# A decoder whose cross attention moves row centring and probability copies to ScalarE and forms its query projection from seven half-size products

## The chip, the cores and the metric

The kernel runs on one core of a Trainium2 chip, in float32 throughout. The metric is the device time of one launch in microseconds (us). Engines are named as in the profile: PE (TensorE: matmuls and transposes; PEld its weight loads), DVE (VectorE), ACT (ScalarE), POOL (GpSimd) and SP (SyncE, whose queue issues every DMA of this kernel).

## The reference, cut to what matters

An encoder layer works on a context of 2 x 77 rows of 512; a decoder layer then works on 2 sequences of 2048 rows of 512, with 16 heads of 32 and a feed-forward width of 2048.

```
y = y + mha(ln1(y), ln1(y), sa_*, causal + relative bias)   # self attention
y = y + mha(ln2(y), memory, ca_*, relative bias)            # cross attention, 77 keys
h = ln3(y)
y = y + relu(h @ ff1_w.T + ff1_b) @ ff2_w.T + ff2_b
```

with `ln(x) = (x - mean) * rsqrt(var + eps) * s + b` on each row, and inside `mha`: `q = (xq @ wq.T + bq) / sqrt(32)`, scores, softmax, times v, output projection. The change lies in the cross attention: how `ln2` and `ln3` centre a row, how its softmax probabilities are brought into the turned layout, and how its `q` is multiplied.

## The kernel before, in words

The rows of the decoder are cut into 8 blocks of 512 (2 sequences x 4), a block into 4 tiles of 128 rows. Every engine's order of work is the order in which the program issues it: nothing is reordered.

The first part, up to about 1757 us, runs 128 units of self attention, with the encoder and the cross attention of block 0 (`first_cross`, slots 65 and on) laid between them in `light`, `late` and `jobs` lists by unit number. `w1_sums` and `w1_store` (L1125, L1137) form sums of quarters of the first feed-forward weight there on POOL, in four units of block 6, and write them to DRAM as `w1_d`.

The second part runs the feed-forward network of blocks 0 to 7. Both of its products are done by halves: a product of 2 x 2 halves takes seven products of halves instead of eight, on sums formed before, and adds them up in PSUM. Such an order is written in `ONE` (L1159): for each of the seven, the weight's half or sum, the half or sum of the rows, the chain of PSUM banks (0 or 1), whether the chain starts afresh, and the output quarter that it then holds. A block has 56 slots (`ff_slot`, L1364): 28 of `first_product` (L1294; 4 matmuls of 128x256) and 28 of `second_product` (L1323; 8 matmuls of 128x128, 4 in every fourth slot). An fp32 matmul is two records in the trace. Slot 0 begins with `sums_n` (L1225), four POOL subtractions of 128x512; `sums_h` (L1260) forms the sums for the second product on DVE and POOL. Weights are streamed by `feed` (L1200) into a ring of 16 places of 256 KB, `w_ring` (L1197), as many tiles ahead as it has places.

Beside the slots of block x, one step ahead of each slot, runs the cross attention of block x + 1 (`cross`, L1386). A list `plan` holds what is issued at each of the 56 steps; so at step n PE, DVE, ACT and POOL first get the entries of `plan[n]`, then slot n. With the stages named as in the code:

- Normalisation `n2` of tile t (`norm_stages`, L732): `stats` at step t (DVE, then the power -1/2 on POOL, L743), `center` at step t + 2 (DVE subtracts the mean and multiplies, L749; POOL then adds a bias row to y, L750), `turned` at step t + 4 (4 transposes on PE, L755, into one bank; 4 activations on ACT scale, shift and copy out, L758).
- The query projection, at steps 9 to 12: `q_group` (L762), 4 matmuls of 128x512 into one bank and one DVE operation (L766) each.
- Attention of tile t, beginning at step 14 + 7t - 1 or 14 + 7t (`attend_stages`, L768): `score` (16 matmuls into 4 banks; DVE subtracts the maximum), `exp` on ACT (L793), `sums` on DVE, `normalize` on POOL (L804), `turned` (L806: four groups of 4 transposes, each group into a bank that is copied out, the even ones by ACT, L814, the odd ones by DVE, L812), `times_v`, `out`. The score of tile 3 is at step 35, one after `turned` of tile 2.
- Normalisation `n3` of tile t, the same three stages, at steps 27, 29 and 31 (+ 7t).

This work takes its PSUM banks in turn from four (`bank`, L179); the feed-forward products have the other four. The cross attention of block 1 begins with its first steps between the last units; those of blocks 2 to 7 run beside the slots of blocks 1 to 6; block 7 has none beside it.

Of the kernel before, what the change touches and what calls it, by code (L numbers as in the profile page):

```python
# [10 lines left out]
F32 = mybir.dt.float32  # L11
AF = mybir.ActivationFunctionType
# [42 lines left out]
def tile_encoder_decoder(ctx: ExitStack, tc: tile.TileContext, ins, out):  # L55
# [5 lines left out]
    def wchunk(name, c0, n=D):  # L61

        return ins[name][:, c0 : c0 + n].rearrange("(c p) o -> p c o", p=P)
# [94 lines left out]
    with (  # L158
# [573 lines left out]
        def norm_stages(y, n, row, place, done):  # L732

            keep = {}

            def stats():
                st = sm.tile([P, 6], F32, name="bnst", tag="bnst")
                mv = sm.tile([P, 2], F32, name="cmv", tag="cmv", bufs=4)
                rs = sm.tile([P, 2], F32, name="crs", tag="crs", bufs=4)
                nc.vector.bn_stats(st, y())  # L740
                nc.vector.bn_aggr(mv, st)
                nc.vector.tensor_scalar_add(rs[:, 0:1], mv[:, 1:2], EPS)
                nc.gpsimd.tensor_tensor(rs[:, 1:2], rs[:, 0:1], mhalf[:, 0:1], ALU.pow)  # L743
                keep.update(mv=mv, rs=rs)

            def center():
                xn = keep["xn"] = place()
                mv, rs = keep["mv"], keep["rs"]
                nc.vector.tensor_scalar(xn, y(), mv[:, 0:1], rs[:, 1:2], ALU.subtract, ALU.mult)  # L749
                nc.gpsimd.tensor_tensor(y(), y(), row, ALU.add)  # L750

            def turned():
                xn, pt, dst = keep["xn"], bank(), done()
                for c in range(NC):
                    nc.tensor.transpose(pt[:, ts(c, P)], xn[:, ts(c, P)], ident)  # L755
                for c in range(NC):
                    sc, bi = vec(f"dec_{n}_s", c), vec(f"dec_{n}_b", c)
                    nc.scalar.activation(dst[:, c, :], pt[:, ts(c, P)], AF.Identity, bias=bi, scale=sc)  # L758

            return stats, center, turned  # L760
# [7 lines left out]
        def attend_stages(q, kTc, v, y, biased, pr, pts, place, w_o, bi=None):  # L768


            prh = pr.rearrange("p (h k) -> p h k", k=S)
            by_r = pr.rearrange("p (g r k) -> p g r k", r=HC, k=S)
            keep = {}

            def score():
                mx = sm.tile([P, NC, HC], F32, name="cmx", tag="cmx", bufs=3)
                banks = [bank() for _ in range(HC)]
                for g in range(NC):
                    for r in range(HC):
                        nc.tensor.matmul(  # L780
                            banks[r][:, ts(g, S)], q(g)[rows4(r)], kTc[rows4(r), g, :], start=True, stop=True
                        )
                for r in range(HC):
                    s = banks[r][:, : NC * S].rearrange("p (g k) -> p g k", k=S)
                    d = by_r[:, :, r, :]
                    if biased:
                        nc.vector.tensor_tensor(d, s, bi[r] if bi else d, ALU.add)
                        s = d
                    nc.vector.tensor_reduce(mx[:, :, r], s, AX.X, ALU.max)
                    nc.vector.tensor_tensor(d, s, mx[:, :, r, None].to_broadcast([P, NC, S]), ALU.subtract)  # L790

            def exp():
                nc.scalar.activation(pr, pr, AF.Exp)  # L793

            def sums():
                su = sm.tile([P, H], F32, name="csu", tag="csu", bufs=2)
                ri = sm.tile([P, H], F32, name="cri", tag="cri", bufs=2)
                nc.vector.tensor_reduce(su, prh, AX.X, ALU.add)
                nc.vector.reciprocal(ri, su)  # L799
                keep["ri"] = ri  # L800

            def normalize():
                ri = keep["ri"]
                nc.gpsimd.tensor_tensor(prh, prh, ri[:, :, None].to_broadcast([P, H, S]), ALU.mult)  # L804

            def turned():  # L806
                for g in range(NC):
                    pt = bank()
                    for r in range(HC):
                        nc.tensor.transpose(pt[:S, ts(r, P)], prh[:, g * HC + r, :], ident)  # L810
                    if g % 2:
                        nc.vector.tensor_copy(pts(g), pt[:S, :])  # L812
                    else:
                        nc.scalar.copy(pts(g), pt[:S, :])  # L814

            def times_v():
                ot = bank()
                for g in range(NC):
                    for r in range(HC):
                        h = g * HC + r  # L820
                        nc.tensor.matmul(
                            ot[rows4(r), ts(g, P)], v[:, ts(h, HD)], pts(g)[:, ts(r, P)], start=True, stop=True
                        )
                keep["oT"] = place()
# [200 lines left out]
        oflat = oT_all.rearrange("p a q -> p (a q)")  # L1025
        pr = oflat[:, : H * S]
        kTcs = [pts_all[:, 4 + b, : NC * S].rearrange("p (c k) -> p c k", k=S) for b in range(B)]
        w_q, vcs, qT = [], [], []

        def big(i):  # L1030
            return vflat[:, i * TB * D : (i + 1) * TB * D]
# [11 lines left out]
        def early_loads():  # L1043
            nc.sync.dma_start(nTt, nT3_d)
            row_into(bv, "dec_ca_out_b")
            for o in range(2):
                w_q.append(small_w(o * P, "dec_ca_in_wT"))
            w_q.append(pts_all[:, 6, :].rearrange("p (c o) -> p c o", c=NC))

        def last_loads():  # L1050
            t = sb.tile([P, MB], F32, name="q", tag="q", bufs=3)
            t = t.rearrange("p (c o) -> p c o", c=NC)
            nc.sync.dma_start(t, wchunk("dec_ca_in_wT", (NC - 1) * P, P))
            w_q.append(t)
            for b in range(B):
                t = sb.tile([P, MB], F32, name="q", tag="q", bufs=3)
                nc.sync.dma_start(t[:S, :], cv_d[:, b, :])
                vcs.append(t)

        def late_loads():  # L1060
            nc.sync.dma_start(w_q[2], wchunk("dec_ca_in_wT", 2 * P, P))
            for t in range(TB):
                new_y(1, t)
            for b in range(B):
                nc.sync.dma_start(kTcs[b], ckT_d[:, :, ts(b, S)])
            for _ in range(2):
                t = sb.tile([P, HC, 2 * P], F32, name="bias", tag="bias", bufs=2)
                qT.append(t.rearrange("p (g a) k -> p g (a k)", g=2))
# [7 lines left out]


        w1_d = dram.tile([4, NC, P, D], F32, name="w1_d")
        w2_d = dram.tile([7, 7, P, D], F32, name="w2_d")
        free = pp[:, 3 * HC * MB : END - 3 * HC * MB]  # L1080
        tens = free.rearrange("p (z q o) -> p z q o", z=8, q=2)
# [40 lines left out]
            for k in range(4):  # L1122
                store(z0, z1, f"T{k + 1}", t[:, k])

        def w1_sums(n):  # L1125

            raw = free[:, : 4 * D].rearrange("p (r k o) -> p r k o", r=2, k=NC)
            got = free[:, 4 * D :].rearrange("p (s k o) -> p s k o", s=4, k=2)
            for r in range(2):
                nc.sync.dma_start(raw[:, r], wchunk("dec_ff1_wT", r * (DFF // 2) + n * TOK, TOK))  # L1130
            a11, a12, a21, a22 = (raw[:, r, 2 * c : 2 * c + 2] for r in range(2) for c in range(2))
            s1, s2, s3, s4 = (got[:, s] for s in range(4))
            gp.tensor_tensor(s1, a21, a22, ALU.add)
# [1 line left out]
            minus(gp, s3, a11, a21)  # L1135
            minus(gp, s4, a12, s2)

        def w1_store(n):
            nc.sync.dma_start(
                w1_d[:, n].rearrange("s p x -> p s x"), free[:, 4 * D :].rearrange("p (s x) -> p s x", s=4)  # L1140
            )

        u = 2 * NU
# [4 lines left out]
            light[u + k].append(lambda c=c: w2_sums(c))  # L1148
        u = 6 * NU
        for n, k in enumerate((0, 2, 4, 10)):  # L1150
            light[u + k].append(lambda n=n: w1_sums(n))
            late[u + k + 1].append(lambda n=n: w1_store(n))

# [40 lines left out]
                    for k in range(7):  # L1194
                        yield w2_d[ON_W2[name], k]

        w_ring = [low[:, j % 4 * T + j // 4 * D : j % 4 * T + j // 4 * D + D] for j in range(16)]  # L1197
        tiles, fed, used = weight_tiles(), [0], [0]

        def feed(upto):  # L1200
# [163 lines left out]
        def ff_slot(s):  # L1364
# [12 lines left out]
            if FIRST <= n < FIRST + TB:  # L1377
                new_y(x + 2, n - FIRST)

        xt_ring, xt_turn = [pts_all[:, 7, :]], [0]  # L1380

        def next_xt():
# [3 lines left out]
        def cross(x):  # L1386
# [9 lines left out]
            for t in range(TB):  # L1396
# [2 lines left out]
                )  # L1399
                for k, f in zip((0, 2, 4), fs):  # L1400
                    plan[t + k].append(f)
            for g in range(NC):
                plan[9 + g].append(lambda g=g: q_group(g, w_q[g], nT2, qT[g // 2][:, g % 2, :]))
            bias_1 = None
            if m == 0:

# [49 lines left out]
        while i < len(stream):  # L1456
# [10 lines left out]
            turn(pair)  # L1467
            if n == end - 2:
                for _, k0, _ in pair:
                    feed(k0 + 4)  # L1470
            turned_to[n] = pair[-1][1] + pair[-1][2]
            if ends and n + 1 < end:
                slot(n + 1)
# [75 lines left out]
```

## Time and profile before

| | us |
|---|---|
| median of 3 runs | 2880.58 (2879.85 to 2881.13) |
| the profiled execution | 2880.44 |
| its span in the trace | 2878.70 |
| first part, about | 1757 |
| one steady block of the second part (q projection to q projection) | 143.9 |
| last block, without cross attention beside it | 101.6 |

The profiled execution lies 0.14 us from the median; 1.74 us of it lie outside the span. The profile gives, for each engine, its busy time, and for each idle stretch what ended it. The start of a record is exact to its 0.01 us, but the end of a matmul is modelled: of two stretches of equal work, the distance from start to start tells which was held up, also where no idle time is named.

### The profile page before, as it was taken

Reading aid. Unit: us, or ns where it says so; the run is one execution under the profiler, and the core shown is the slowest. Engines: PE = TensorE matmul, PEld = TensorE weight load, DVE = VectorE, ACT = ScalarE, POOL = GpSimd, SP = SyncE. Lnnn points to the kernel's source line nnn. Section 1 sums busy time; section 2 is a strip of 40 time slices with the busy share of each in tenths; the row PEclk is TensorE's granted clock in tenths of the full one; section 3 lists DMA queues with packets and bytes.
Section 4 is the critical chain, followed back from the end, with each engine's and each line's share of the span. In section 5 each row is a group of like instructions: output and inputs, shape, how many; then the busy total and the mean of one; then the engine's idle time right before and its main releaser. Section 6 shows DMA issues by size and latency. Waiting matters only on the chain.

```text
span 2878.7 us, 64333 instructions
## 1 busy us (share of the span) xinstructions
PE 2827.8 (98%) x25782; PEld 2041.2 (71%) x25782; DVE 2033.3 (71%) x5550; ACT 1296.5 (45%) x2455; POOL 737.3 (26%) x573
## 2 busy tenths in 40 slices
PE   9899999999999999999999999999999999999998
PEld 5557666666666556666666677888888888888888
DVE  4767688878986678788878894666666666666645
ACT  3344465456665446555546674323232323232321
POOL 0100050200000101020000002363636363636355
PEclk9899999999999999999999999999999999999999
DMA  6413443401111502232301115454546454545365
GB/s 174 116 32 123 122 135 101 121 18 45 35 42 57 143 23 68 71 105 69 89 16 38 38 35 188 131 182 130 182 131 198 130 182 131 181 132 180 116 201 182
DMA packets 251773, 316.16 MB, mean 110 GB/s; under 512 B 29472, under 2 KB 142672, under 8 KB 251346
## 3 DMA queue, kind: packets, MB, share of 16 engines
q1 hardware_dynamic: 251474, 312.05, 35.9%
q8 instruction: 203, 3.33, 0.5%
q14 instruction: 96, 0.79, 0.1%
HBM read 273.07 MB, written 38.90 MB: 108 GB/s over the span
## 4 chain that ended last, share of the span: by engine, by line
PE 81%; DVE 8%; POOL 4%; ACT 3%; issue 3%; DMA 1%; SPq 0%; POOLq 0%; DVEq 0%; ACTq 0%
PE psum L425 17%; PE psum L371 11%; PE psum L1303 10%; PE psum L442 9%; PE psum L1332 7%; PE psum L765 4%; PE psum L215 4%; PE psum L239 4%; PE psum L251 4%; PE psum L226 3%; PE psum L830 3%; DVE pp L1090 2%; PE psum L780 1%; PE psum L810 1%; ACT pp L402 1%
## 5 line engine op out<-in xcount | busy, mean ns | idle before, releaser
L402 ACT ACTIVATE pp<-pp,nm 128x128 f32<-128x128 f32 (+15 forms) x512 | 611.6, 1201 | 265.6 <-DVE nm L397 265.3
L380 DVE TENSOR_SCALAR_CACHE_REDUCE pp<-psum 128x512 f32<-128x512 f32 (+3 forms) x1024 | 559.2, 590 | 58.2 <-PE psum L371 56.7
L425 PEld LDWEIGHTS psum<-ident,pp 128*128 128x128 f32 x4352 | 475.3, 142 | 110.1 <-DVE pp L380 50.8
L425 PE MATMUL psum<-ident,pp 128*128 128x128 f32 x4352 | 537.6, 278 | 8.3 <-DVE mx L387 3.8
L431 ACT COPY pts<-psum 128x512 f32<-128x512 f32 (+3 forms) x592 | 298.1, 575 | 474.9 <-PE psum L425 368.8
L429 DVE COPY pts<-psum 128x512 f32<-128x512 f32 (+2 forms) x544 | 330.0, 659 | 68.2 <-PE psum L425 67.9
L371 PE MATMUL psum<-kT,q 32*128 32x512 f32 (+3 forms) x2560 | 362.4, 578 | 7.1 <-ACT pts L431 4.5
L442 PEld LDWEIGHTS psum<-pts,vv 128*32 128x32 f32 x8704 | 227.3, 110 | 126.1 <-issue 117.3
L1332 PE MATMUL psum<-pp 128*128 128x128 f32 x2560 | 306.4, 276 | 1.9 <-POOL pp L1090 1.6
L1332 PEld LDWEIGHTS psum<-pp 128*128 128x128 f32 x2560 | 295.8, 192 | 17.4 <-issue 10.6
L442 PE MATMUL psum<-pts,vv 128*32 128x128 f32 x8704 | 280.9, 277 | 0.7 <-ACT pts L431 0.6
L1303 PE MATMUL psum<-vv,pp 128*128 128x256 f32 x1024 | 238.5, 381 | 0.0
L371 PEld LDWEIGHTS psum<-kT,q 32*128 32x128 f32 x2560 | 125.7, 184 | 143.6 <-issue 88.6
L1303 PEld LDWEIGHTS psum<-vv,pp 128*128 128x128 f32 x1024 | 189.8, 190 | 32.2 <-issue 8.4
L387 DVE CUSTOM_DVE_ANT_0 pp<-psum,bias 128x256 f32<-128x256 f32 (+1 forms) x512 | 195.9, 411 | 16.4 <-PE psum L371 16.4
L1090 POOL TENSOR_TENSOR pp<-pp 128x512 f32<-128x512 f32 x124 | 171.6, 1399 | 105.2 <-DMA pp<-in_dec_ff_wT_dram 91.2
L285 POOL TENSOR_TENSOR rstd<-rstd,mhalf 128x1 f32<-128x1 f32 x32 | 18.2, 570 | 668.1 <-DVE rstd L284 668.1
L1319 ACT ACTIVATE kT<-kT,vecs 128x256 f32<-128x256 f32 x192 | 87.7, 508 | 219.3 <-DVE kT L1316 219.2
L1303 PE MATMUL psum<-nT,pp 128*128 128x256 f32 x768 | 173.4, 379 | 0.0
L1303 PEld LDWEIGHTS psum<-nT,pp 128*128 128x128 f32 x768 | 145.3, 190 | 28.6 <-issue 10.2
L804 POOL TENSOR_TENSOR oT<-oT,cri 128x1232 f32<-128x1232 f32 x28 | 67.7, 2418 | 353.8 <-DVE cri L799 353.8
L1316 DVE TENSOR_TENSOR kT<-kT,psum 128x512 f32<-128x512 f32 x96 | 65.7, 686 | 119.1 <-PE psum L1303 89.7
(188 smaller groups left out, 3703.9 us busy)
## 6 DMA issues: line engine op xcount, KB each, us to landing
pp<-w_d SPq DMA_DIRECT2D x520, 256.0 KB, 2.9
pp<-in_dec_ff_wT_dram SPq DMA_DIRECT2D x112, 256.0 KB, 3.8
wqk<-in_dec_sa_in_wT_dram SPq DMA_DIRECT2D x64, 256.0 KB, 3.7
bias<-tzg SPq DMA_DIRECT2D x128, 128.0 KB, 3.7
wbig<-in_dec_sa_in_wT_dram SPq DMA_DIRECT2D x8, 1024.0 KB, 6.6
vv<-in_enc_ff_wT_dram SPq DMA_DIRECT2D x8, 1024.0 KB, 5.3
wbig<-in_dec_sa_out_wT_dram SPq DMA_DIRECT2D x8, 1024.0 KB, 6.6
vv<-y SPq DMA_DIRECT2D x32, 256.0 KB, 5.5
```

The costliest lines, as they stand in the source:

```text
L215: nc.tensor.matmul(mm, w[:, c, :], nTs[b, m][:, c, :], start=(c == 0), stop=(c == NC - 1))
L371: nc.tensor.matmul(banks[r][:, : kn * P], q[rows4(r), ts(t, P)], kT[rows4(r), g, k0 * P : (k0 + kn) * P], start=True, stop=True,)
L380: nc.vector.tensor_scalar(p[:, k0 * P : (k0 + far) * P], s[:, : far * P], 1.0, None, ALU.mult, ALU.max, accum_out=st["mx"][:, r, c : c + 1],)
L387: nc.vector.tensor_tensor_reduce(p[:, (i + 1) * P - w : (i + 1) * P], s[:, far * P : kn * P], biases[b, m, g][:, r, 2 * P - w :], 1.0, LOW ...
L402: nc.scalar.activation(p, p, AF.Exp, bias=nm, accum_out=to)
L425: nc.tensor.transpose(pt[:, ts(x, P)], state[n]["p"][r][:, ts(k, P)], ident)
L429: nc.vector.tensor_copy(pts[:, : len(load), :], pt[:, :w])
L431: nc.scalar.copy(pts[:, : len(load), :], pt[:, :w])
L442: nc.tensor.matmul(ot[rows4(r), t, :], vv[:, k, ts(g * HC + r, HD)], got.pop((n, k, r)), start=(k == 0), stop=(k == i),)
L1090: engine.tensor_tensor(out, a, b, ALU.subtract)
L1303: nc.tensor.matmul(mm[:, ts(f, TOK)], a[:, c, ts(f, P)], b[:, c, :], start=fresh and f == 0 and c == 0, stop=c == 1, skip_group_check=True,)
L1332: nc.tensor.matmul(psum[:, bank_i, ts(col, P)], lhs[:, c, :], w[:, c, :], start=fresh and k in (0, 3) and c == 0, stop=c == 3, skip_group_ ...
```

## The change

- `center` becomes an activation on ACT, `rstd * y + (-mean * rstd)`. `stats` therefore gets one more POOL operation on 128x1 values, behind the power, that forms `-mean * rstd`.
- `turned` in `attend_stages` copies all four groups by ACT.
- `q_group` stays for block 0. For blocks 1 to 7 the query projection follows the list `ONE`: four sums of halves of the rows on POOL at step 8, and seven products at steps 9 (two), 10 (two), 11 (two) and 12 (one), each of 4 matmuls of 128x256. The four quarters written first are copied out by two ACT activations each, the three added later by one DVE operation each.
- The sums of the weight's halves are formed once, by the same `w1_sums` in unit 108, and stored by `w1_store` at the end of unit 109. Their tiles lie in SBUF all through the second part: three of them in the last three places of the weight ring, which now has 13.
- `late_loads` issues four loads for the query weight in front of its others, where it issued one.
- One DVE operation at the start forms the scaled bias.

```diff
 def stats():
-    rs = sm.tile([P, 2], F32, name="crs", tag="crs", bufs=4)
+    rs = sm.tile([P, 3], F32, name="crs", tag="crs", bufs=4)
...
     nc.gpsimd.tensor_tensor(rs[:, 1:2], rs[:, 0:1], mhalf[:, 0:1], ALU.pow)
+    nc.gpsimd.tensor_scalar(rs[:, 2:3], mv[:, 0:1], rs[:, 1:2], -1.0, ALU.mult, ALU.mult)
...
 def center():
-    nc.vector.tensor_scalar(xn, y(), mv[:, 0:1], rs[:, 1:2], ALU.subtract, ALU.mult)
+    nc.scalar.activation(xn, y(), AF.Identity, bias=rs[:, 2:3], scale=rs[:, 1:2])
     nc.gpsimd.tensor_tensor(y(), y(), row, ALU.add)
...
-                    if g % 2:
-                        nc.vector.tensor_copy(pts(g), pt[:S, :])
-                    else:
-                        nc.scalar.copy(pts(g), pt[:S, :])
+                    nc.scalar.copy(pts(g), pt[:S, :])
...
 def late_loads():
-    nc.sync.dma_start(w_q[2], wchunk("dec_ca_in_wT", 2 * P, P))
+    for n in ("S2", "S3", "S4", "22"):
+        load_w_q(n)
...
+light[u + 12].append(lambda: w1_sums("dec_ca_in_wT", TOK, 0))
+late[u + 13].append(lambda: w1_store(wq_d))
...
-w_ring = [low[:, j % 4 * T + j // 4 * D : j % 4 * T + j // 4 * D + D] for j in range(16)]
+w_ring = [low[:, j % 4 * T + j // 4 * D : j % 4 * T + j // 4 * D + D] for j in range(13)]
...
+def q_sums():
+    minus(gp, of_q("T1"), of_q("12"), of_q("11"))
+    minus(gp, of_q("T2"), of_q("22"), of_q("T1"))
+    minus(gp, of_q("T3"), of_q("22"), of_q("12"))
+    minus(gp, of_q("T4"), of_q("21"), of_q("T2"))
+
+def q_product(j, banks):
+    name, by, chain, fresh, to = ONE[j]
+    if fresh:
+        banks[chain] = bank()
+    mm, b = banks[chain], of_q(by)
+    a = w_q[name].rearrange("p (c o) -> p c o", c=2)
+    for f in range(2):
+        for c in range(2):
+            nc.tensor.matmul(
+                mm[:, ts(f, TOK)], a[:, c, ts(f, P)], b[:, c, :],
+                start=fresh and f == 0 and c == 0, stop=(c == 1), skip_group_check=True,
+            )
+    got = mm.rearrange("p (f n) -> p f n", f=2)
+    r, c = int(to[0]) - 1, int(to[1]) - 1
+    dst = qT[r][:, :, ts(c, TOK)]
+    if to in [p[4] for p in ONE[:j]]:
+        ve.scalar_tensor_tensor(dst, got, SCALE, dst, ALU.mult, ALU.add)
+        return
+    for f in range(2):
+        g = 2 * r + f
+        nc.scalar.activation(dst[:, f], got[:, f], AF.Identity, bias=q_bias[:, g : g + 1], scale=SCALE)
...
-            for g in range(NC):
-                plan[9 + g].append(lambda g=g: q_group(g, w_q[g], nT2, qT[g // 2][:, g % 2, :]))
+            plan[8].append(q_sums)
+            for j in range(len(ONE)):
+                plan[9 + j // 2].append(lambda j=j: q_product(j, q_banks))
```

More of the change, by code (lines that the diff above doesn't have):

```diff
@@ L743, in stats @@
                 nc.gpsimd.tensor_tensor(rs[:, 1:2], rs[:, 0:1], mhalf[:, 0:1], ALU.pow)
-                keep.update(mv=mv, rs=rs)
+                nc.gpsimd.tensor_scalar(rs[:, 2:3], mv[:, 0:1], rs[:, 1:2], -1.0, ALU.mult, ALU.mult)
+                keep.update(rs=rs)
             def center():
                 xn = keep["xn"] = place()
-                mv, rs = keep["mv"], keep["rs"]
-                nc.vector.tensor_scalar(xn, y(), mv[:, 0:1], rs[:, 1:2], ALU.subtract, ALU.mult)
+                rs = keep["rs"]
+                nc.scalar.activation(xn, y(), AF.Identity, bias=rs[:, 2:3], scale=rs[:, 1:2])
                 nc.gpsimd.tensor_tensor(y(), y(), row, ALU.add)
@@ L1027, in tile_encoder_decoder, with load_w_q @@
         kTcs = [pts_all[:, 4 + b, : NC * S].rearrange("p (c k) -> p c k", k=S) for b in range(B)]
-        w_q, vcs, qT = [], [], []
+        w_q, vcs, qT = {}, [], []
+        w_q.update({n: low[:, (j + 1) * T + 3 * D : (j + 2) * T] for j, n in enumerate(("S3", "S4", "22"))})
+        def load_w_q(n):
+            if n[0] == "S":
+                nc.sync.dma_start(w_q[n], wq_d[int(n[1]) - 1])
+            else:
+                r, c = int(n[0]) - 1, int(n[1]) - 1
+                nc.sync.dma_start(
+                    w_q[n].rearrange("p (c o) -> p c o", c=2),
+                    ins["dec_ca_in_wT"][c * TOK : (c + 1) * TOK, r * TOK : (r + 1) * TOK].rearrange(
+                        "(c p) o -> p c o", p=P
+                    ),
+                )
         def big(i):
@@ L1045, in early_loads @@
             row_into(bv, "dec_ca_out_b")
-            for o in range(2):
-                w_q.append(small_w(o * P, "dec_ca_in_wT"))
-            w_q.append(pts_all[:, 6, :].rearrange("p (c o) -> p c o", c=NC))
+            for n in ("11", "12"):
+                w_q[n] = sb.tile([P, NC, P], F32, name="wqk", tag="wqk", bufs=2).rearrange("p c o -> p (c o)")
+                load_w_q(n)
+            w_q["S2"] = pts_all[:, 6, :]
         def last_loads():
[L1051 to L1054, printed above, removed]
+            w_q["S1"] = sb.tile([P, MB], F32, name="q", tag="q", bufs=3)
+            load_w_q("S1")
             for b in range(B):
@@ L1060, in late_loads @@
         def late_loads():
-            nc.sync.dma_start(w_q[2], wchunk("dec_ca_in_wT", 2 * P, P))
+            for n in ("S2", "S3", "S4", "22"):
+                load_w_q(n)
             for t in range(TB):
@@ L1078, in tile_encoder_decoder @@
         w1_d = dram.tile([4, NC, P, D], F32, name="w1_d")
+        wq_d = dram.tile([4, P, D], F32, name="wq_d")
         w2_d = dram.tile([7, 7, P, D], F32, name="w2_d")
@@ L1123, in w2_store, with w1_sums @@
                 store(z0, z1, f"T{k + 1}", t[:, k])
-        def w1_sums(n):
+        def w1_sums(name, step, n):
             raw = free[:, : 4 * D].rearrange("p (r k o) -> p r k o", r=2, k=NC)
@@ L1129, in w1_sums @@
             for r in range(2):
-                nc.sync.dma_start(raw[:, r], wchunk("dec_ff1_wT", r * (DFF // 2) + n * TOK, TOK))
+                nc.sync.dma_start(raw[:, r], wchunk(name, r * step + n * TOK, TOK))
             a11, a12, a21, a22 = (raw[:, r, 2 * c : 2 * c + 2] for r in range(2) for c in range(2))
@@ L1136, in w1_sums, with w1_store @@
             minus(gp, s4, a12, s2)
-        def w1_store(n):
+        def w1_store(dst):
             nc.sync.dma_start(
-                w1_d[:, n].rearrange("s p x -> p s x"), free[:, 4 * D :].rearrange("p (s x) -> p s x", s=4)
+                dst.rearrange("s p x -> p s x"), free[:, 4 * D :].rearrange("p (s x) -> p s x", s=4)
             )
@@ L1150, in tile_encoder_decoder @@
         for n, k in enumerate((0, 2, 4, 10)):
-            light[u + k].append(lambda n=n: w1_sums(n))
-            late[u + k + 1].append(lambda n=n: w1_store(n))
+            light[u + k].append(lambda n=n: w1_sums("dec_ff1_wT", DFF // 2, n))
+            late[u + k + 1].append(lambda n=n: w1_store(w1_d[:, n]))
+        light[u + 12].append(lambda: w1_sums("dec_ca_in_wT", TOK, 0))
+        late[u + 13].append(lambda: w1_store(wq_d))
         ONE = (
@@ L1378, in ff_slot, with of_q @@
                 new_y(x + 2, n - FIRST)
+        q_bias = const.tile([P, NC], F32, name="q_bias")
+        nc.vector.tensor_scalar(q_bias, vecs[:, _COL["dec_ca_in_b"] : _COL["dec_ca_in_b"] + NC], SCALE, None, ALU.mult)
+        t_q = high[:, NC * MB : 2 * NC * MB].rearrange("p (t c o) -> p t c o", t=4, c=2)
+        def of_q(name):
+            if name[0] == "T":
+                return t_q[:, int(name[1]) - 1]
+            r, c = int(name[0]) - 1, int(name[1]) - 1
+            return nT2[:, 2 * r : 2 * r + 2, ts(c, TOK)]
+        def q_sums():
[14 more added lines that the diff above has]
+                        start=fresh and f == 0 and c == 0, stop=(c == 1), skip_group_check=True,
+                    )
+            got = mm.rearrange("p (f n) -> p f n", f=2)
[7 more added lines that the diff above has]
+                nc.scalar.activation(dst[:, f], got[:, f], AF.Identity, bias=q_bias[:, g : g + 1], scale=SCALE)
         xt_ring, xt_turn = [pts_all[:, 7, :]], [0]
@@ L1401, in cross @@
                     plan[t + k].append(f)
-            for g in range(NC):
-                plan[9 + g].append(lambda g=g: q_group(g, w_q[g], nT2, qT[g // 2][:, g % 2, :]))
+            plan[8].append(q_sums)
+            q_banks = {}
+            for j in range(len(ONE)):
+                plan[9 + j // 2].append(lambda j=j: q_product(j, q_banks))
             bias_1 = None
@@ L1469, in tile_encoder_decoder @@
                 for _, k0, _ in pair:
-                    feed(k0 + 4)
+                    feed(min(k0 + 4, len(w_ring)))
             turned_to[n] = pair[-1][1] + pair[-1][2]
```

## The prediction

> **What bounds the kernel now.** I read the page's first two parts, then the table of busy times by stretch, then the PE timeline of one block.
>
> ```profile
> PE 2827.8 (98%) x25782; PEld 2041.2 (71%) x25782; DVE 2033.3 (71%) x5550; ACT 1296.5 (45%) x2455; POOL 737.3 (26%) x573
> PEclk9899999999999999999999999999999999999999
> ```
>
> PE is busy 98% of the span, at full clock. Less work for PE is therefore time, and freeing DVE is time only where PE waits for DVE. The part that changes most is one block of the second part (columns: stretch, us, busy and count of PE, PEld, DVE, ACT, POOL, then clock, DMA share, GB/s):
>
> ```profile
> 2076.70:2220.60 143.90, 141.74 (x1033) 116.34 (x1033) 88.67 (x151) 45.21 (x100) 73.83 (x53) 1.00 0.54 159
> ```
>
> ACT has room on average. The PE timeline of such a block (start, length, count; idle before it and who ended that) shows the two places where PE is held:
>
> ```profile
> 1936.34 1.89 PE L1303 MATMUL psum<-vv,pp 128*128 128x256 f32 x8
> 1938.07 3.60 PE L765 MATMUL psum<-pp,wqk 128*128 128x512 f32 x8
> 1941.50 1.89 PE L1303 MATMUL psum<-nT,pp 128*128 128x256 f32 x8
> ...
> 2008.01 1.95 PE L1332 MATMUL psum<-pp 128*128 128x128 f32 x16
> 2009.89 0.44 PE L780 MATMUL psum<-pts,bias 32*128 32x77 f32 x2
> 2010.65 0.45 PE L780 MATMUL psum<-pts,bias 32*128 32x77 f32 x4 [0.32 <-DVE pts L812]
> 2011.25 1.11 PE L780 MATMUL psum<-pts,bias 32*128 32x77 f32 x26
> 2012.29 2.94 PE L1332 MATMUL psum<-pp 128*128 128x128 f32 x24
> ...
> 2065.16 1.89 PE L1303 MATMUL psum<-vv,pp 128*128 128x256 f32 x8
> 2068.14 0.66 PE L755 MATMUL psum<-ident,pts 128*128 128x128 f32 x4 [1.08 <-DVE pts L749]
> ```
>
> From start to start, four 128x256 matmuls (8 records) cost 1.73 us and four 128x512 cost 3.43. The score of tile 3 takes 2.40 us (2009.89 to 2012.29); the score of tile 0 takes 1.06 (1953.64 to 1954.70). So 1.34 us are lost there, behind DVE's copies. At 2068.14 the transposes of tile 1 wait for its centring. Why that is late stands on POOL's timeline:
>
> ```profile
> 2060.41 0.55 POOL L743 TENSOR_TENSOR crs<-crs,mhalf 128x1 f32<-128x1 f32 x1
> 2060.92 1.27 POOL L1090 TENSOR_TENSOR vv<-nT 128x512 f32<-128x512 f32 x1
> ...
> 2066.02 0.55 POOL L743 TENSOR_TENSOR crs<-crs,mhalf 128x1 f32<-128x1 f32 x1
> 2066.53 1.26 POOL L750 TENSOR_TENSOR vv<-vv,row_sa_bv 128x512 f32<-128x512 f32 x1
> ```
>
> Tile 1's power stands behind the four subtractions of slot 0, and DVE's centring (2066.60, 1.48 us) behind it.
>
> **Part 1, the products: 11.9 us less.** Before, 4 groups: 3.54 (1932.80 to 1936.34) + 3 x 3.43 = 13.83 us. After, 7 products x 1.73 = 12.11. That is 1.7 us a block, in blocks 1 to 7: 7 x 1.7 = 11.9. All of it is PE time on the path. The weight loads stay covered: 0.19 us each under 0.216 of matmul, as in L1303. What comes with it:
> - Four POOL subtractions, 4 x 1.27 = 5.1 us. POOL stood idle 32.81 us before L804 (2105.97), so they hide. The third product needs the second of them; it has two products and a slot, 3.45 + 1.73 = 5.2 us, against 2.6 of POOL. If POOL were late, PE would wait what is missing.
> - Copies out: 8 activations (0.47 each, L1319 from PSUM) on ACT, 3 DVE operations (0.75, as L766; bounds 0.69, L1316, and 1.8, the slowest two-input row here) for 4 of 0.75. Each has a slot of 1.73 us before its bank is taken again: nothing.
> - The sums of weights: two loads, 4 POOL operations (5.1 us) and a store, between 1400 and 1500 us, where POOL is busy 0.00; on SP the store waits for POOL, as the four like it do, for which PE's waits name nothing. Three more loads in front of block 1's rows: 0.4 us of issue each, and PE has the output projections there. Both 0; together at most 2 us.
> - The ring. In the second half a tile is used every 0.9 us, so 13 places are 11.6 us ahead and 16 were 14.3; a tile lands 2.9 us after issue. Nothing; were the lead short, up to 3 x 0.9 = 2.7 us a block.
>
> **Part 2, probability copies: 9.4 us less.** ACT now makes four copies, 0.58 each and about 0.49 apart (L814). Behind `turned` of tile 2, ACT is idle from 2005.84, so it starts at 2006.90 and ends by about 2009.0; PE comes at 2009.89. The loss of 1.34 goes; the table of waits counts it 7 times, once a block: 9.4 us. At the other two tiles ACT ends 0.5 us (step 28) and 0.9 us (step 21) before PE comes. Bounds: 0, if what follows (DVE's and POOL's sums for the second product) doesn't move up with PE, and 9.4. I take 9.4, since POOL's next gap (2.42 us, before 2017.09) ends on a DVE operation queued behind this very score.
>
> **Part 3, centring on ACT: 5.5 us more.** Two new costs are in no row. The POOL operation on 128x1: between 0.10 (a 128x1 memset) and 1.11 (the longest L743); widths 384 and 512 of L1090 (1.01, 1.28) leave 0.2 for no elements, L743 itself is 0.55. I take 0.4, between those two, with its wait. The activation, 128x512 with two operands of one column: L758 at width 128 has both and takes 0.485; L402 grows 0.32 from 128 to 512 (0.39, 0.71): 0.80, between 0.58 (L814) and 1.23 (L793). DVE's own takes 0.54 alone and 1.45 (its median) where POOL runs beside it.
>
> The Trainium skill, page "ScalarE: Activation LUTs", section "Rules for kernel authors", says to leave additions and multiplications to VectorE rather than ScalarE. By that rule each of the 56 centrings would lose 0.80 - 0.54 = 0.26 us of latency; with the median of this trace, 1.45, it gains 0.65. Its "GPSIMD Engine Reference", "Specifications", names an SBUF interface that GpSimd shares with VectorE, which agrees with the two durations.
>
> Now `n2` in the block at 2057.81, on POOL's clock. Two more 0.4 lie before tile 1's value: 2066.57 becomes 2067.4. ACT's centring of tile 1 ends at 2068.25, and PE's transposes start at 2068.35 instead of 2068.14. But ACT works in order. Behind that centring stand slot 3's two relus (0.91), the 4 activations of tile 0 (1.49), then tile 2's centring: done at 2071.25. PE comes at 2068.35 + 0.44 + 1.73 = 2070.5 and waits 0.8. Then a copy (0.5), tile 1's activations (1.49) and tile 3's centring: 2073.9; PE comes at 2073.5 and waits 0.5. The two slots after it end at 2077.9, where q started at 2076.70 before: 1.2 us later, 6 blocks: 7.2 us more. (Block 1 has the output projections between these steps: 0.)
>
> `n3`: tile 2's transposes at 2036.48 come 0.7 us after PE could (2035.78). POOL's 0.4 more, ACT's 0.8 instead of DVE's 1.49: 0.3 less, 6 blocks: 1.7 us less.
>
> Block 0's cross attention, in the first part, moves 8 x (0.80 + 0.58) = 11 us to ACT, where PE waits for ACT 4.1 us in all, and takes 8 x (0.54 + 0.68) = 10 us off DVE: 0, between -3 and +3.
>
> **Sum.** -11.9 - 9.4 + 7.2 - 1.7 = -15.8 us. 2880.44 - 15.8 = 2864.6; the median of the runs shown is 0.14 above the profiled execution.
>
> **Rivals.**
> 1. *Only the products count.* The score's 1.34 is lost again further on, because POOL's and DVE's sums don't move up. For: POOL runs almost without gaps from 2002 to 2044. Against: its gaps end on DVE, which gets freer. Then -11.9 + 7.2 - 1.7 = -6.4, 2874; with more waiting, up to 2879.
> 2. *The waits of `n2` go too.* If ACT's queue is ahead of my count (relus earlier, the 128x1 operation at 0.1), of the 1.2 a block nothing is left and the old 1.4 goes: 6 x 2.6 = 15.6 less, 2849. Against: 2.6 us of ACT per step against 2.17 of PE.
> 3. *Slower: POOL's chain sets the pace.* At 1.1 a piece, the 128x1 operation delays `n2` by 2 x 0.7 = 1.4 more, and two of them in the crowded second half, where tile 3's transposes already start 0.2 us behind POOL's L804, delay PE by 2.2; the score's gain goes too. Per block -1.7 + 2.6 + 2.2 = +3.1, x 6 = 18.6, less 1.7 for block 1: 2897. It decides from about 0.8 us an operation.
> 4. *The change does less than it says*: were 128x256 matmuls here slower than in L1303 because their operands come late, part 1 falls towards 0: 2876.
>
> **How the numbers follow.** Forecast 0.52 (2858 to 2870), rival 2 0.17 (2845 to 2858), rivals 1 and 4 together 0.22 (2870 to 2880), rival 3 0.09. The range from 2849 to 2878 leaves out rival 3 and the ends of rivals 2 and 1: under 2 in 10. A difference of 0.2%, 5.8 us, is about what a measurement of this kernel can tell from no change; that is below 2874.8. Half of rivals 1 and 4 lies there: faster 0.52 + 0.17 + 0.11 = 0.80, same 0.11, slower 0.09.
>
> **What would show it.** The PE timeline: seven starts 1.73 apart where q is; the score of tile 3 taking 1.06; waits of L755 that name ACT instead of DVE, about 1.4 + 0.8 + 0.5 us a block, ahead of tiles 1, 2 and 3; the steady block at 143.9 - 1.7 - 1.3 + 1.2 - 0.3 = 141.8 us. PE waits for POOL in L1332, or for a DMA in L1303, would speak for rival 3 or the ring. I am wrong first if the 128x1 operation is not near 0.4, or if ACT's order lets other work in front of the centrings.

## The result and the profile after

| | before | after |
|---|---|---|
| median (4 runs each), us | 2880.86 (2879.85 to 2881.19) | 2860.48 (2857.88 to 2861.54) |
| ratio, 95% interval | 1 | 0.9928 (0.9914 to 0.9942) |
| profiled execution / its span, us | 2880.44 / 2878.70 | 2861.14 / 2859.2 |
| steady block, q to q, us | 143.89 | 140.92 (one of six: 141.28) |

The change takes 20.4 us (0.72%) off the median, where 15.8 were forecast. The busy row of the page and the granted clock, after:

```profile
PE 2811.5 (98%) x25950; PEld 2070.5 (72%) x25950; DVE 1924.1 (67%) x5416; ACT 1395.4 (49%) x2639; POOL 782.0 (27%) x669
PEclk9899999999999999999999999999999999999999
```

PE lost 16.3 us of busy time though it has 168 more records, since they are of half the width. DVE lost 109 us and ACT gained 99: of that only the little for which PE had waited can show in the time. The table by stretch, for the same block as before (it is the one of 141.28):

```profile
2072.21:2213.49 141.28, 139.17 (x1057) 120.21 (x1056) 74.62 (x133) 58.02 (x124) 78.75 (x66) 1.00 0.56 163
```

The PE timeline after (L1317 and L1346 are the feed-forward products, L1419 the query projection, L781 the score, L756 the transposes of a normalisation):

```profile
1931.30 3.62 PE L1419 MATMUL psum<-pp,wqk 128*128 128x256 f32 x16
1934.75 1.89 PE L1317 MATMUL psum<-vv,pp 128*128 128x256 f32 x8
1936.48 1.89 PE L1419 MATMUL psum<-pp,pts 128*128 128x256 f32 x8
...
2006.63 1.13 PE L781 MATMUL psum<-pts,bias 32*128 32x77 f32 x32
2007.70 2.94 PE L1346 MATMUL psum<-pp 128*128 128x128 f32 x24
...
2059.82 1.89 PE L1317 MATMUL psum<-vv,pp 128*128 128x256 f32 x8
2062.80 0.66 PE L756 MATMUL psum<-ident,pts 128*128 128x128 f32 x4 [1.08 <-ACT pts L750]
2063.29 1.89 PE L1317 MATMUL psum<-vv,pp 128*128 128x256 f32 x8
2065.69 0.66 PE L756 MATMUL psum<-ident,xt 128*128 128x128 f32 x4 [0.50 <-ACT xt L750]
2066.18 1.89 PE L1317 MATMUL psum<-vv,pp 128*128 128x256 f32 x8
2068.26 0.66 PE L756 MATMUL psum<-ident,xt 128*128 128x128 f32 x4 [0.19 <-ACT xt L750]
```

The first product group holds two products (16 records) and lasts 3.45 us from start to start, the next ones 1.73 each. The score of tile 3 takes 1.07 us in one piece, where DVE had broken it up. And PE waits for ACT ahead of tile 1, and now ahead of tiles 2 and 3 as well. The whole table of PE's waits between 1780 and 2800 us (us in total, times, longest):

```profile
PE psum L756 <- ACT xt L750: 7.2, 12, 1.1
PE psum L756 <- ACT pts L750: 3.6, 6, 1.1
PE psum L811 <- POOL oT L805: 0.3, 1, 0.3
```

18 of these waits are three in each of six blocks: 1.08, 0.50 and 0.19. What they rest on is on POOL's timeline, and behind it ACT's:

```profile
2060.98 0.55 POOL L743 TENSOR_TENSOR crs<-crs,mhalf 128x1 f32<-128x1 f32 x1
2061.63 0.27 POOL L744 TENSOR_SCALAR crs<-cmv,crs 128x1 f32<-128x1 f32 x1
```
```profile
2061.93 0.81 ACT L750 ACTIVATE pts<-vv,crs 128x512 f32<-128x512 f32 x1 [2.37 <-POOL crs L744]
2062.65 0.89 ACT L1333 ACTIVATE kT<-kT,vecs 128x256 f32<-128x256 f32 x2
2063.45 1.48 ACT L759 ACTIVATE pp<-psum,vecs 128x128 f32<-128x128 f32 x4
2064.82 0.81 ACT L750 ACTIVATE xt<-vv,crs 128x512 f32<-128x512 f32 x1
```

ACT was idle for 2.37 us until POOL's new operation (L744) ended; then the relus and tile 0's activations stand between the centrings of tile 1 and tile 2, in just the order that the prediction wrote out.

### The profile page after: what moved, and what is told of

It reads as the page before. It is cut to its first block, busy times and chain, and to the rows that moved or that the text cites. A ratio compares the mean times of both kernels' runs of the same rounds, so it can differ in the third digit from the quotient of the medians.

```text
span 2859.2 us, 65017 instructions
## 1 busy us (share of the span) xinstructions
PE 2811.5 (98%) x25950; PEld 2070.5 (72%) x25950; DVE 1924.1 (67%) x5416; ACT 1395.4 (49%) x2639; POOL 782.0 (27%) x669
## 4 chain that ended last, share of the span: by engine, by line
PE 89%; DVE 4%; ACT 3%; POOL 2%; issue 1%; DMA 1%; SPq 0%; POOLq 0%; DVEq 0%; ACTq 0%
PE psum L425 17%; PE psum L1346 11%; PE psum L1317 11%; PE psum L371 11%; PE psum L442 9%; PE psum L215 4%; PE psum L239 4%; PE psum L828 4%; PE psum L251 4%; PE psum L226 3%; PE psum L1419 3%; PE psum L811 2%; PE psum L781 1%; ACT pp L402 1%; PE psum L819 1%
## 5 line engine op out<-in xcount | busy, mean ns | idle before, releaser
L1346 PEld LDWEIGHTS psum<-pp 128*128 128x128 f32 x2560 | 295.8, 192 | 17.4 <-issue 11.4
L1346 PE MATMUL psum<-pp 128*128 128x128 f32 x2560 | 306.4, 276 | 1.9 <-POOL pp L1102 1.6
L1102 POOL TENSOR_TENSOR pp<-pp 128x512 f32<-128x512 f32 x155 | 209.7, 1370 | 120.0 <-DMA pp<-in_dec_ff_wT_dram 100.4
L1317 PE MATMUL psum<-vv,pp 128*128 128x256 f32 x1024 | 238.5, 381 | 0.0
L1317 PEld LDWEIGHTS psum<-vv,pp 128*128 128x128 f32 x1024 | 189.8, 190 | 26.3 <-issue 1.9
L387 DVE CUSTOM_DVE_ANT_0 pp<-psum,bias 128x256 f32<-128x256 f32 (+1 forms) x512 | 196.0, 411 | 16.3 <-PE psum L371 16.3
L1317 PE MATMUL psum<-nT,pp 128*128 128x256 f32 x768 | 173.4, 379 | 0.0
L1317 PEld LDWEIGHTS psum<-nT,pp 128*128 128x128 f32 x768 | 145.3, 190 | 22.6 <-issue 3.5
L805 POOL TENSOR_TENSOR oT<-oT,cri 128x1232 f32<-128x1232 f32 x28 | 67.7, 2418 | 283.3 <-DVE cri L800 258.4
```

The source lines that it names most:

```text
L387: nc.vector.tensor_tensor_reduce(p[:, (i + 1) * P - w : (i + 1) * P], s[:, far * P : kn * P], biases[b, m, g][:, r, 2 * P - w :], 1.0, LOW ...
L1102: engine.tensor_tensor(out, a, b, ALU.subtract)
L1317: nc.tensor.matmul(mm[:, ts(f, TOK)], a[:, c, ts(f, P)], b[:, c, :], start=fresh and f == 0 and c == 0, stop=c == 1, skip_group_check=True,)
L1346: nc.tensor.matmul(psum[:, bank_i, ts(col, P)], lhs[:, c, :], w[:, c, :], start=fresh and k in (0, 3) and c == 0, stop=c == 3, skip_group_ ...
```

## The experiments

The theory at the outset: the three parts are separate pieces of PE's path and add up, the centring being a loss. The rival: the parts share the relief of DVE, so that one part alone would bring most of it, or none of it. Later the question was narrower: what makes `n2` wait, ACT's queue or POOL's order?

To read them all alike I cut a steady block by starts of PE's work (us; `n3` of tile 1 lies between `times_v` and `out` of tile 2, `n3` of tile 2 between those of tile 3). What is not listed is 78.2 in every kernel.

| stretch of a block | before | after | centring alone | copies alone | products alone | all but centring | centring at `n3` only |
|---|---|---|---|---|---|---|---|
| q start to first score | 20.83 | 19.09 | 20.74 | 20.84 | 19.09 | 19.09 | 19.08 |
| score of tile 3 | 2.42 | 1.07 | 2.11 | 1.06 | 2.40 | 1.06 | 1.06 |
| with `n3` of tile 1 | 5.13 | 5.12 | 5.12 | 5.32 | 5.13 | 5.31 | 5.12 |
| next, to `times_v` of tile 3 | 12.69 | 12.61 | 12.43 | 13.18 | 12.70 | 13.18 | 12.62 |
| with `n3` of tile 2 | 5.76 | 5.12 | 5.74 | 5.12 | 5.77 | 5.12 | 5.12 |
| `n2`: slot 0 to q | 18.89 | 19.74 | 19.74 | 18.88 | 18.60 | 18.61 | 18.61 |
| block | 143.89 | 140.92 | 144.04 | 142.58 | 141.86 | 140.56 | 139.80 |

**The centring alone**, added to the kernel before:

```diff
+    nc.gpsimd.tensor_scalar(rs[:, 2:3], mv[:, 0:1], rs[:, 1:2], -1.0, ALU.mult, ALU.mult)
...
-    nc.vector.tensor_scalar(xn, y(), mv[:, 0:1], rs[:, 1:2], ALU.subtract, ALU.mult)
+    nc.scalar.activation(xn, y(), AF.Identity, bias=rs[:, 2:3], scale=rs[:, 1:2])
```

> The kernel before, with the centring alone moved to ACT (and the 128x1 POOL operation it needs). Theory of separate terms: the waits ahead of n2's transposes grow by 0.75 us a block, as between the two traces (6 x 0.75 = 4.5 more), those ahead of n3's tile 2 go (7 x 0.6 = 4.2 less), the score of tile 3 keeps its loss of 1.34: within 2 us of the kernel before, 2881. Rival (DVE and POOL freed are what pays): 5 to 10 us faster, 2871 to 2876, with the score of tile 3 shorter.

Measured: 2880.76 (11 runs) against 2880.35; ratio 1.0000 (0.9991 to 1.0009); block +0.15. No difference in the time, but not an idle edit: `n2` loses 0.85 a block, and the score and the turning of tile 3 gain 0.31 and 0.26, with DVE relieved of the centring. `n3` of tile 2, where the forecast had seen a gain, gains nothing (5.76 to 5.74).

**The copies alone**, added to the kernel before:

```diff
-                    if g % 2:
-                        nc.vector.tensor_copy(pts(g), pt[:S, :])
-                    else:
-                        nc.scalar.copy(pts(g), pt[:S, :])
+                    nc.scalar.copy(pts(g), pt[:S, :])
```

> The kernel before, with the probability copies alone all on ACT. Theory of separate terms: the loss of 1.34 us at the score of tile 3 goes in 7 blocks, 9.4 us less, 2871; n2's wait of 1.08 that names DVE stays. Rival (the score's gain is lost again behind DVE and POOL unless the centring moves too): 0 to 4 us less, with more or longer waits further on in the block.

Measured: 2871.79 (2870.68 to 2872.10); 0.9968 (0.9956 to 0.9981); block -1.31. The score gives 1.36. `n3` of tile 2 gives 0.64, and so does not need the centring on ACT. Its cause is on the timelines; first DVE and POOL with the centring alone, where the odd copies are still DVE's:

```profile
2030.82 1.27 DVE L813 COPY pts<-psum 77x512 f32<-77x512 f32 x2
```
```profile
2030.99 2.84 POOL L1352 TENSOR_TENSOR vv<-vv,oT 128x512 f32<-128x512 f32 x1
```

and POOL's same operation with the copies alone, where ACT makes them:

```profile
2028.75 1.72 POOL L1348 TENSOR_TENSOR vv<-vv,oT 128x512 f32<-128x512 f32 x1
```

Beside DVE's two copies, POOL's addition takes 2.84 us; without them 1.72. Tile 2's power stands behind it on POOL. In the kernel before it takes 2.84 as well, and DVE then waits 1.68 us for the power (DVE's two lines, POOL's between them):

```profile
2029.70 1.27 DVE L812 COPY pts<-psum 77x512 f32<-77x512 f32 x2
2029.87 2.84 POOL L1351 TENSOR_TENSOR vv<-vv,oT 128x512 f32<-128x512 f32 x1
2034.94 1.49 DVE L749 TENSOR_SCALAR pts<-vv,cmv,crs 128x512 f32<-128x512 f32 x1 [1.68 <-POOL crs L743]
```

Two other places take 0.19 and 0.49 back. The second is named in the PE timeline of this kernel, where tile 3's probabilities now wait for their normalisation on POOL:

```profile
2025.49 1.97 PE L810 MATMUL psum<-ident,oT 128*77 128x128 f32 x16 [0.53 <-POOL oT L804]
```

**The products alone**, with the ring of 13, the sums and the loads that belong to them:

```diff
-                plan[9 + g].append(lambda g=g: q_group(g, w_q[g], nT2, qT[g // 2][:, g % 2, :]))
+            plan[8].append(q_sums)
+                plan[9 + j // 2].append(lambda j=j: q_product(j, q_banks))
```

> The kernel before, with the query projection alone in seven products (and the ring of 13 places, the sums of weights and the loads that go with it). Theory of separate terms: 7 x 1.75 = 12.2 us less, 2868.5; waits as in the kernel before. Rival (four more POOL operations and three places less in the ring cost something): 4 to 8 us less, with PE waits that name POOL or a DMA in the feed-forward products.

Measured: 2867.38 (2865.85 to 2868.90); 0.9953 (0.9939 to 0.9967); block -2.03. The products give 1.74. Another 0.29 lies ahead of them: the first two products need only the first half of the rows ("11" and "21" in `ONE`), so that q no longer waits for tile 3's activations (in the kernel before it starts at 2076.70, 0.29 behind the two slots ahead of it).

**All but the centring**, and **the ring alone** (the kernel before with 13 places, the last three left empty):

```diff
-    nc.scalar.activation(xn, y(), AF.Identity, bias=rs[:, 2:3], scale=rs[:, 1:2])
+    nc.vector.tensor_scalar(xn, y(), mv[:, 0:1], rs[:, 1:2], ALU.subtract, ALU.mult)
```

> The changed kernel with the centring put back on DVE, so copies and products without it. Theory of separate terms: the centring is worth about nothing, so 2859 to 2861, as the changed kernel; n2 waits once for DVE, 1.08 us, and n3's tile 2 again by 0.4. Rival (the centring frees DVE and POOL, which the others need): 2866 to 2870.

> The kernel before with a ring of 13 weight tiles instead of 16, and nothing else (the three places stay empty). Theory: 11.6 us of lead against 3 us to land, so a block of 143.9 and 2880 to 2882. Rival (the lead is needed): waits of PE for a DMA in the feed-forward products, up to 2.7 us a block.

Measured: without the centring 2857.87 (2853.16 to 2859.55); 0.9918 (0.9905 to 0.9932); block 140.56, 0.36 shorter than in the change as made. The ring of 13: 2881.01 (10 runs) against 2881.84; 0.9995 (0.9986 to 1.0005); block 143.89, no wait for a DMA: it costs nothing. (Only its first block differs, 144.51; it holds a stretch at a granted clock of 0.50, shown in the last section.) So the change is held back by its own third part, but by 0.36 a block, not by the 0.9 that the forecast charged.

**The centring at one place only** (`n2` stays on DVE, `n3` on ACT):

```diff
+                if n == "n3":
                     nc.scalar.activation(xn, y(), AF.Identity, bias=rs[:, 2:3], scale=rs[:, 1:2])
+                else:
+                    nc.vector.tensor_scalar(xn, y(), mv[:, 0:1], rs[:, 1:2], ALU.subtract, ALU.mult)
```

> The changed kernel with the centring of n2 back on DVE and that of n3 left on ACT. If the centring on ACT costs at n2 (2.27 us lost ahead of the transposes against 1.25) and pays at n3 and behind it (0.58 us: the transposes of tile 3 wait 0.54 for POOL's normalisation in the kernel without the centring on ACT, and hardly in the changed one), a block takes 140.0 instead of 140.9, and the kernel about 2855. Rival (both places alike): 2858 to 2861.

Measured: 2853.06 (2852.32 to 2853.30) against 2881.66; 0.9903 (0.9887 to 0.9920); block 139.80. From the last two columns of the table, the centring on ACT is worth 0.76 at `n3`; from this column and that of the change, it costs 1.12 at `n2`. Where the 0.76 comes from stands on the two timelines of the kernel without it, DVE first, then POOL:

```profile
2152.03 0.54 DVE L749 TENSOR_SCALAR xt<-vv,cmv,crs 128x512 f32<-128x512 f32 x1
2152.48 4.03 DVE L1101 TENSOR_TENSOR pp<-kT,pp 128x512 f32<-128x512 f32 x3
```
```profile
2156.05 1.59 POOL L1283 TENSOR_TENSOR pp<-pp 128x512 f32<-128x512 f32 x1 [0.69 <-DVE pp L1101]
2157.72 1.27 POOL L1101 TENSOR_TENSOR pp<-pp 128x512 f32<-128x512 f32 x1
2158.95 2.70 POOL L804 TENSOR_TENSOR oT<-oT,cri 128x1232 f32<-128x1232 f32 x1
```

The centring of tile 1 stands on DVE in front of three sums (L1101); POOL is idle for 0.69 us for their result, and L804, for which PE waits, stands behind that. With the centring on ACT the idle time is gone, and L804 (there L805) starts 0.75 us earlier in the block (87.89 against 88.64 after q). The same operations in the change as made, whose q starts at 1931.30:

```profile
2016.15 1.72 POOL L1284 TENSOR_TENSOR pp<-pp 128x512 f32<-128x512 f32 x1
2017.95 1.27 POOL L1102 TENSOR_TENSOR pp<-pp 128x512 f32<-128x512 f32 x1
2019.18 2.70 POOL L805 TENSOR_TENSOR oT<-oT,cri 128x1232 f32<-128x1232 f32 x1
```

**POOL's new operation three times over** (the same value written three times), to see whether POOL sets `n2`'s pace:

```diff
-                nc.gpsimd.tensor_scalar(rs[:, 2:3], mv[:, 0:1], rs[:, 1:2], -1.0, ALU.mult, ALU.mult)
+                for _ in range(3):
+                    nc.gpsimd.tensor_scalar(rs[:, 2:3], mv[:, 0:1], rs[:, 1:2], -1.0, ALU.mult, ALU.mult)
```

> The changed kernel with its 128x1 POOL operation done three times over (the same value each time). If POOL's chain sets n2's pace, the two operations before the subtractions and the two before tile 1's centring cost 4 x 0.37 = 1.5 us more a block: 142.4, 9 us more, about 2869, and waits at n3 may come on top. Rival (ACT's own order sets the pace): a block of at most 141.3, at most 2 us more.

Measured: 2872.09 (2871.97 to 2873.57) against 2881.84; 0.9966 (0.9954 to 0.9979); blocks of 142.9 to 143.3. POOL's three, and PE behind them:

```profile
2205.98 0.99 POOL L745 TENSOR_SCALAR crs<-cmv,crs 128x1 f32<-128x1 f32 x3
```
```profile
2207.86 0.66 PE L757 MATMUL psum<-ident,xt 128*128 128x128 f32 x4 [2.52 <-ACT xt L751]
```

0.99 instead of 0.27 us is 0.72 more; two of them lie ahead of tile 1's value, and the wait went from 1.08 to 2.52, that is by 2 x 0.72. The wait bears ACT's name and is POOL's. That is most of the 2.0 us by which a block grows (140.92 to 142.9); 0.34 more is lost at `n3` of tile 2 and 0.18 at `n2`'s tile 3. The longer blocks have other causes: the third has a wait of 0.3 for POOL's normalisation, as the 141.28 of the change has, and in each of the last three the trace shows 3.4 us at a granted clock of 0.50 within `n2`.

**The statistics of `n2`'s tiles 1 to 3 one step earlier**, so that tile 1's stand ahead of slot 0's four subtractions on POOL; first in the change as made, then with the centring back on DVE:

```diff
-                for k, f in zip((0, 2, 4), fs):
+                for k, f in zip((0 - (t > 0), 2, 4), fs):
```

> The changed kernel, with the statistics of n2's tiles 1, 2 and 3 one step earlier (steps 0, 1, 2), so that tile 1's power and 128x1 operation stand on POOL in front of slot 0's four subtractions. If POOL's order is what holds the centring of tile 1 and, through ACT's order, of tiles 2 and 3, the three waits (2.3 us by starts) go: a block of 138.6 instead of 140.9, 6 x 2.3 = 14 us less, about 2847. Rival (ACT has too much to do at these steps: 2.6 us a step against PE's 2.17): the wait only moves to tiles 2 and 3, a block of 140 or more, 2855 or more.

> The same earlier statistics, with the centring on DVE (copies and products as changed). If POOL's order holds tile 1, its wait (1.25 us by starts) goes: a block of 139.3 instead of 140.6, 7.5 us less than without, about 2850. Rival (DVE beside POOL, 1.45 us a centring, is the limit): the wait moves to tiles 2 and 3, 2856 or more.

Measured: 2847.09 (2845.74 to 2848.66) against 2881.84; 0.9879 (0.9864 to 0.9894); block 138.93. It is the best of all kernels run here. With the centring on DVE: 2850.29 (2846.43 to 2850.50); 0.9887 (0.9872 to 0.9902); block 139.37. POOL's timeline in the first of them:

```profile
2053.47 0.55 POOL L743 TENSOR_TENSOR crs<-crs,mhalf 128x1 f32<-128x1 f32 x1
2054.12 0.27 POOL L744 TENSOR_SCALAR crs<-cmv,crs 128x1 f32<-128x1 f32 x1
2054.34 1.27 POOL L1102 TENSOR_TENSOR vv<-nT 128x512 f32<-128x512 f32 x1
```

Tile 1's pair now ends before the first subtraction (L1102) instead of behind the fourth. The waits that are left:

```profile
PE psum L756 <- ACT xt L750: 0.8, 4, 0.2
PE psum L756 <- ACT pts L750: 0.4, 2, 0.2
PE psum L811 <- POOL oT L805: 0.3, 1, 0.3
```

The stretch of `n2` falls from 19.74 to 17.73, to 17.40 with DVE. So once POOL's order is mended, the centring on ACT costs 0.33 at `n2` and still saves 0.76 at `n3`: it has become a gain of 0.44 a block (2.6 us in six blocks; the two medians differ by 3.2, with ranges that overlap, so the sizes rest on the blocks).

**Both kernels once more**, one execution each:

> The kernel before once more, unchanged, for its trace. If the 1.4 us by which the changed kernel reaches the first query projection of the second part later (1790.37 against 1788.98) is scatter of the first part, this execution's own start of it differs by as much, 1785 to 1791, with blocks of 143.9. Rival (the change costs it): 1789.0 again within 0.3.

> The changed kernel once more, unchanged, for its trace. As scatter: the first query projection of the second part starts anywhere from 1785 to 1791, with blocks of 140.9. Rival (the change costs the first part 1.4 us): 1790.4 again within 0.3.

Measured: before 2876.92, after 2862.11. The blocks repeat to 0.03 us (143.9; 140.94 and one of 141.28). The start of block 1's q, which stands for the first part, does not: 1785.46 against 1788.98 of the first trace of before, 1791.29 against 1790.37 after.

## Why the prediction came out as it did

It was right in sign, and in mechanism but for `n3`; the time of 2860.48 lies 4.1 us under the 2864.6 forecast. In the profile the 19.5 us of the span are 17.38 in the six steady blocks (1788.98 to 2652.26 became 1790.37 to 2636.27), 3.51 behind the last q, and 1.39 lost ahead of block 1's q. Step by step, per block:

- **Products, -1.7**: -1.74. Seven starts 1.73 apart, no wait for POOL's sums or a DMA.
- **Copies, -1.34**: -1.35 at the score. The doubt whether POOL's and DVE's sums would follow was to the point: with the copies alone they do not quite (0.49 lost at L804).
- **`n2`, +1.2**: +0.85. The order on ACT's queue was as written out; the waits were mis-sized. The new POOL operation takes 0.27 us and lengthens POOL's chain by 0.36 (0.87 from the start of a power to what follows the pair, where it was 0.51), near the 0.4 charged. Relative to slot 0 the value of tile 1 comes 0.67 later, where 0.83 was reckoned, and ACT's centring is as much shorter than DVE's 1.48, so the wait at tile 1 stays at 1.08, where PE was to come 0.2 later. The other two are 0.67 and 0.35 by starts (0.50 and 0.19 as the profile names them), where 0.8 and 0.5 were forecast.
- **`n3`, -0.3**: -0.64 in the change, and here the reason failed: it was credited to the centring, but the centring alone gives 0.02 and the copies alone 0.64, by the 1.12 us that POOL's addition loses beside DVE's copies. What the centring does at `n3`, removing 0.19 and 0.56 of waits that the copies bring in, no step of the prediction had.
- **Turning of tile 3**, not in the sum: -0.08.
- **Sums of weights, loads, ring, block 0: 0**. The ring is shown to cost nothing. For the rest there is no sign: the interval of block 0's cross attention (706 to 1758 us) differs by 0.2 us between the two first traces.

-1.74 - 1.35 + 0.85 - 0.64 - 0.08 = -2.96, against -2.97 measured and -2.14 forecast. Five blocks have it; the one of 141.28 has 0.4 less, and the mean of the six is 17.38 / 6 = 2.90. The missing 0.76 x 6 = 4.5 us are `n2` (0.35) and `n3` (0.34), then the turning of tile 3 (0.08). Behind the last q, 3.51 stand against 1.7 + 1.34; ahead of block 1's q, the 1.39 are within what two executions of one kernel differ by (3.5, above). The step that failed is part 3, with 5.5 us of net loss: its two stretches measure 0.85 - 0.64 = 0.21 a block, 1.3 us in six. And the 0.64 is not the centring's: taken out of the change as made, the centring costs 0.36 a block, 2.2 us.

The theory that the parts add holds nearly in the total, and not by stretches: alone they give +0.15, -1.31 and -2.03, together -3.19 against -2.97. Gained twice in that sum are 0.29 ahead of q (with the centring alone q does not wait for tile 3's activations either, so its 0.85 is already net of it), 0.32 at the score of tile 3, 0.18 at the turning of tile 3 and 0.09 behind q; against them, the copies' losses of 0.19 and 0.49 are gone when the centring is on ACT too. That the totals come so near is the chance of these nearly cancelling.

**The rivals.** The first (the score's gain lost again) and the fourth (slow 128x256 products) are refuted by the table. The second (`n2`'s waits vanish) did not come; what makes them vanish is not a quicker ACT queue, as it had it, but POOL's order. Its price, 2849, is nearly that of the kernel with the early statistics, 2847.1. The third, POOL's chain, has the right mechanism: the threefold operation shows its slope, two links for each delay. Its price was wrong: at 0.99 us, above its point of 0.8, a block is still 0.6 to 1.0 shorter than before, not 3.1 longer, since the gain at the score stays and `n3` loses 0.34 instead of 2.2.

The runs decide on the rule weighed in the prediction, that of the Trainium skill's "ScalarE: Activation LUTs", "Rules for kernel authors", to leave additions and multiplications to VectorE. By length alone it is right: 0.81 us on ACT against 0.54 on an undisturbed DVE. (The median of DVE's 64 in the trace before is 1.22, not 1.45; the disturbed ones have 1.44 to 1.53.) What decided was the queue: the same move gains 0.76 at `n3` and costs 1.12 or 0.33 at `n2`, depending on POOL's order.

What stays open: why one block in six has the extra 0.3 us wait for L805 (it begins at DVE, whose first L791 of tile 3's score waits 0.46 us for POOL's L744 in that block alone), and what the sums and loads of weights cost in the first part, whose scatter is larger than the 2 us allowed for them. Neither was tried.

## What to carry to other kernels

A wait is named after the last engine of its chain; before moving work to or from that engine, follow the chain to the small operation that stands behind large ones in an in-order queue: here issuing the statistics of three tiles one step earlier, which puts one pair of 128x1 operations in front of four subtractions, was worth about 13 us (12 by the blocks), against 20.4 for the whole change. Price a moved operation at each place where it is issued, by the queue it leaves and the one it joins, since its own length said nothing on the sign. And where a product is split, look at what its first piece needs: it may start before the last operand is there.

## What was not expected of the hardware

- POOL's `tensor_scalar` on 128x1 takes 0.27 us and starts 0.10 after the power that feeds it; its longest is 0.72, the power's 1.00 against 0.55. ACT's 128x512 with two operands of one column takes 0.80 to 0.84 wherever it stands, while DVE's centring takes from 0.53 to 1.53.
- POOL's addition of 128x512 takes 1.27 us undisturbed, 1.72 beside DVE's sums and 2.84 beside its copies out of PSUM: an engine that is freed speeds up the other, and here that was the gain at `n3` of tile 2.
- At the centring, the later of DVE and POOL is the one that is held. In the trace before, DVE's centring takes 0.54 us in the 14 cases where a 128x512 operation of POOL starts 0.16 after it, and POOL's then 1.51 or 1.52 instead of 1.27; it takes 1.44 to 1.53 in the 32 cases where POOL's started 0.03 to 0.11 ahead, and POOL's then stays at 1.27.
- Ahead of block 1's q, executions differ by up to 6.6 us, whatever the kernel. In the thirteen traces of this study, three with a granted clock of 1.00 between 500 and 800 us (the second of the kernel before, the ring of 13, early statistics with DVE) reach that q at 1784.7 to 1785.5; the ten with 0.98 or 0.99 there reach it at 1788.5 to 1791.3. That is more than the parts of 2 to 3 us spoken of here, which is why they were read from the blocks and not from the totals. The clock falls in short stretches: in the ring of 13 it is 0.50 from 1865.2 to 1868.5 us, and the 24 records of L1332 there take 4.50 us from start to start, where 2.87 is usual.
